# Media attention: fillers on TensorE pinned to program order, and the routing of a row spread over more steps

## The chip, the cores and the metric

The kernel runs on one core of a Trainium2 chip. A core has TensorE (matrix multiply; PE in the profile, and PEld for its weight loads), VectorE (DVE), ScalarE (ACT), GpSimd (POOL) and SyncE (SP, which here only starts DMAs), each with an instruction queue of its own that is worked off in order. The metric is the device time of one execution in microseconds, as the median of several runs.

## The reference

The program is a two-layer decoder on an input of 8 rows (batch entries) of 512 tokens with 256 channels. Six blocks follow one another, each with a residual sum: self-attention, cross-attention, local attention with a feed-forward part, quantized attention, attention to media (a context of 512 tokens), and a mixture of experts. The change concerns the fifth block and the routing of the sixth:

```python
# media attention: 8 heads of 64
xn = (x - mu) * rsqrt(var + eps) * gamma + beta
q = xn @ Wq * scale;  k, v = split(media @ Wkv)
attn = softmax(where(mask, q @ k.T, -inf))
x = x + (attn @ v) @ Wout

# experts: routing of T = 4096 tokens to 8 experts of capacity 512
logits = layernorm(x) @ router_w
expert_idx = argmax(logits);  gate = softmax(logits)[expert_idx]
pos = cumsum(onehot(expert_idx))[token, expert_idx] - 1
keep = pos < 512
expert_in[expert_idx, pos] = layernorm(x) * keep
```

The position of a token inside its expert is a running count over all tokens before it, so the rows are routed one after the other.

## The kernel before, in words

The blocks run as stages. The stage of the change is `stage_media_attention` (line 2745); it takes the eight rows `b` in turn, and beside them, as background work, it routes each finished row to the experts.

**The main line.** A row has 512 queries and 512 keys, and its 8 heads are taken as 4 pairs `c`. The loop at line 2905 goes through 64 steps (its variable is `pair`) and one more to finish, eight to a row, called steps 0 to 7 of a row here; two steps make one pair of heads. In a step, `scores` (matmuls at line 2811) makes the scores of two blocks of 128 keys into two PSUM tiles `sc`, ScalarE takes their exponential (line 2817), and the exponentials are summed over the key blocks into `ma_esum`: GpSimd copies the first (line 2822), VectorE adds the others (line 2824). Then `weigh` (line 2835) multiplies the exponentials of the step before with the values. At the end of an odd pair of heads the sums are added up over the partitions by a matmul (line 2854, `SUM` below), go through DRAM to be inverted and spread (`inverted`, `times_rows`, lines 3163 and 3181), and GpSimd multiplies the output by them (line 3189). After `weigh`, the step runs fillers.

**The fillers.** There are two sources. The generator `prepare` gives the next row's work, one piece at a time: load and layer norm, two transposes (line 2781, `mT`), four projections of the queries (line 2791). The object `later`, of class `Background` (line 3235), holds pieces with a due time. It counts ticks, two to a step, 16 to a row; `later.tick(2)` runs up to two pieces that are due and moves the count on. `later.add(d, f)` makes `f` due `d` ticks from now.

**The routing.** When the output projection of a row (four pieces, line 2892, `PO`) is done, `route` (line 2962) adds its pieces to `later`: `stats` (the write of `x` to the output, and the statistics of the layer norm, lines 143 to 149 and 1460 to 1464), `norm` (four normalizations, line 157, into `mo_rows`; a copy of `x` on GpSimd, line 2982), `turn` twice (four PE transposes each, line 2992, `rT0` and `rT1`, and a copy on ScalarE, line 2995), `logits` (line 3001), `choose` (eight small VectorE operations and one exponential), `count` (two matmuls, lines 3032 and 3033), `place` (thirteen small VectorE operations), and four times `send` (an indirect DMA from GpSimd, line 3064). `count` keeps its PSUM tile until `place` has read it. All fillers on TensorE share two PSUM tiles `pj`.

**What sets the order.** The kernel is written in program order, and the framework that builds it chooses the order of each engine's queue: an instruction that the framework believes to be ready may go ahead of one written before it. `tc.issue_after(ins)` makes whatever its block issues on the engine of `ins` stand behind `ins` in that queue; it is an order and no wait for `ins` to finish. `together` (line 1448) uses it so that the four matmuls of `scores`, `weigh` or `SUM` stand side by side. After the eighth row what is left in `later` is drained, one piece a tick (line 3251), and `stage_moe` (line 3094) loads the first expert's tokens, which the last `send` must have written.

Of the kernel before, what the change touches and what calls it, by code (L numbers as in the profile page):

```python
# [40 lines left out]
B, S, C = 8, 512, 256  # L41
# [1236 lines left out]
class FastDecoder(Decoder):  # L1278
# [164 lines left out]
    def reserve(self, pool, *tiles):  # L1443

        for tag, shape, bufs in tiles:
            self.alloc(pool, shape, F32, tag, bufs=bufs)

    def together(self, n):


        yield 0
        last = next(i for i in reversed(self.nc.cur_bb.bb.instructions) if i.engine == mybir.EngineType.PE)
        with self.tc.issue_after(last), self.tc.high_priority(self.AT_ONCE):
            yield from range(1, n)
# [1290 lines left out]
    def stage_media_attention(self, w, out):  # L2745
# [4 lines left out]
        later = Background()  # L2750
        with self.tc.tile_pool(reuse_waits="tile", name="ma", bufs=2) as pool, self.tc.tile_pool(
# [50 lines left out]
            def scores(n):  # L2802

                b, rest = divmod(n, 8)
                c, kts = rest // 2, (2 * (rest % 2), 2 * (rest % 2) + 1)
                d = held[b]
                both = [self.alloc(psum, [P, 2, 512], F32, "sc", bufs=2) for kt in kts]
                for m in self.together(4):
                    kt, r = kts[m // 2], m % 2
                    rows = slice(64 * r, 64 * r + 64)  # L2810
                    nc.tensor.matmul(  # L2811
                        both[m // 2][:, r, :], d["k"][rows, c, kt * P : (kt + 1) * P], d["q"][rows, c, :],
                        start=True, stop=True,
                    )
                for kt, ps in zip(kts, both):
                    ex = d[4 * c + kt] = self.alloc(pool, [P, 2, 512], F32, "ma_e", bufs=4)
                    nc.scalar.activation(  # L2817
                        ex, ps, AF.Exp, bias=bias[:, b * NST + kt : b * NST + kt + 1], scale=0.125
                    )
                    if kt == 0:  # L2820
                        d["sum", c] = self.alloc(pool, [P, 2, 512], F32, "ma_esum", bufs=3)
                        nc.gpsimd.tensor_copy(d["sum", c], ex)
                    else:
                        nc.vector.tensor_tensor(d["sum", c], d["sum", c], ex, ALU.add)  # L2824
# [80 lines left out]
            for pair in range(0, n + 2, 2):  # L2905
                if pair < n:
                    if pair % 16 == 0:
                        for thunk in ready or ():
                            thunk()
                        ready = prepare(pair // 16 + 1) if pair // 16 + 1 < B else iter(())  # L2910
                    scores(pair // 2)
                if pair >= 2:
                    weigh(pair // 2 - 1)
                for i in (pair, pair + 1):
                    if i % 16 > 0:
                        thunk = next(ready, None)
                        if thunk is not None:
                            thunk()
                    later.tick(2)
            later.drain()  # L2920

    def twice_normal(self, pool, b, kept=None):
# [20 lines left out]
    def routing(self, pool, psum, later, out):  # L2943
# [18 lines left out]
        def route(b):  # L2962
# [26 lines left out]
            def turn(c):  # L2989
                ps = self.alloc(psum, [P, 512], F32, "pj", bufs=2)  # L2990
                for i in range(NST):
                    nc.tensor.transpose(  # L2992
                        ps[:, i * P : (i + 1) * P], d["rows"][:, i, c * P : (c + 1) * P], self.ident
                    )
                nc.scalar.copy(d["xnT"][:, c, :], ps)
# [67 lines left out]
            def send(i):  # L3063
                ins = nc.gpsimd.indirect_dma_start(
                    self.slots, bass.IndirectOffsetOnAxis(ap=d["to"][:, i : i + 1], axis=0),
                    d["rows"][:, i, :], None, bounds_check=NEXP * CAP - 1, oob_is_err=False,
                ).ins

                for other in self.sent:
                    if i == 0:  # L3070
                        self.wait_for(ins, other)
                    else:
                        self.tc.declare_no_dep(ins, other, reason="other slots")
                self.sent = [ins] if i == 0 else self.sent + [ins]

            later.add(1, stats)
            later.add(2, norm)
            later.add(3, lambda: turn(0))
            later.add(4, lambda: turn(1))
            later.add(5, logits)  # L3080
            later.add(6, choose)
            later.add(8, count)
            later.add(9, place)
            for i in range(NST):
                later.add(10 + i, lambda i=i: send(i))

        return route

# [357 lines left out]
```

## Time and profile before

| what | value |
|---|---|
| median of three runs | 3141.81 us (3141.59 to 3142.07) |
| the profiled execution | 3142.42 us |
| its span | 3140.5 us, so 1.9 us lie around it |
| PE busy over the span | 2861.4 us (91%) |
| DVE, ACT, POOL busy | 2156.3, 1146.1, 401.6 us |
| main line of the media stage | 2439.4 to 2863.0 us of the span |
| PE, DVE, ACT, POOL busy there | 403.2, 293.6, 172.4, 106.5 us of 423.6 |
| transposes `rT` there, PE idle ahead of them | 13.2 us in 7 waits |

A busy share is an average over the whole span. The media stage is a stretch of 424 us of it, and its time is read from what TensorE does in this stretch: how long it computes, and what it waits for. An fp32 matmul shows as two records, so four matmuls of `scores` are "x8" in a timeline. Where a group of matmuls starts later than the end of the one before it, the idle time and what ended it stand in brackets.

### The profile page before, as it was taken

To read this page: it belongs to the slowest core of one execution; us is meant where nothing else is said; L and a number is where in the kernel's file an instruction comes from. 1 tells how busy PE (TensorE), PEld (TensorE's weight loads), DVE (VectorE), ACT (ScalarE), POOL (GpSimd) and SP (SyncE) were. 2 spreads that over 40 slices of the span, in tenths; PEclk is the share of its full clock that TensorE was granted. 3 is DMA by queue.
4 is the path that set the end of the run, shared out by engine and by line. 5 is a ranking of instruction groups with operands and counts; after the bars stand their busy time and mean duration, and the time that the engine had idled before them with its cause. 6 is when DMAs were issued, how large, how long until landed. Compare 5 with 4: busy or idle time off the path is not lost. (4 is left out here: it accounts for less than half of the span.)

```text
span 3140.5 us, 40216 instructions
## 1 busy us (share of the span) xinstructions
PE 2861.4 (91%) x14944; PEld 1511.3 (48%) x14944; DVE 2156.3 (69%) x4962; ACT 1146.1 (36%) x1607; POOL 401.6 (13%) x389
## 2 busy tenths in 40 slices
PE   8998889887999999999999999998796999997998
PEld 5652222223555556655555556654444344444665
DVE  7458888887878796356788798648788866656110
ACT  2236656652434431124434431113363434341111
POOL 1111000100110010000110011111201123221111
PEclk9999999989999999999999999999997999998999
DMA  7011111111000001001000011001332122223331
GB/s 238 1 49 48 51 59 47 26 32 47 22 29 15 22 24 42 1 1 35 22 22 15 23 43 61 21 7 61 99 127 93 42 88 95 75 75 97 101 137 60
DMA packets 130696, 168.74 MB, mean 54 GB/s; under 512 B 51760, under 2 KB 79665, under 8 KB 128442
## 3 DMA queue, kind: packets, MB, share of 16 engines
q1 hardware_dynamic: 126394, 154.48, 15.8%
q0 software_dynamic: 4096, 11.59, 1.0%
q8 instruction: 119, 1.95, 0.3%
q14 instruction: 87, 0.71, 0.1%
HBM read 113.12 MB, written 47.50 MB: 51 GB/s over the span
## 5 line engine op out<-in xcount | busy, mean ns | idle before, releaser
L1812 PE MATMUL pj<-w,la_hT 128*128 128x512 f32 x720 | 341.0, 613 | 31.5 <-DVE x L1989 15.5
L1664 DVE TENSOR_TENSOR x_e<-x_e,x_share 128x1024 f32<-128x1024 f32 x256 | 306.8, 1244 | 28.5 <-ACT x_e L1663 27.7
L1663 ACT ACTIVATE x_e<-sc 128x1024 f32<-128x1024 f32 x256 | 249.7, 1025 | 149.8 <-PE sc L1652 147.3
L1812 PEld LDWEIGHTS pj<-w,la_hT 128*128 128x128 f32 x720 | 130.6, 192 | 187.0 <-issue 118.1
L1934 ACT ACTIVATE la_e<-la_e 128x1024 f32<-128x1024 f32 (+1 forms) x128 | 121.1, 953 | 212.0 <-DVE la_e L1930 212.0
L2817 ACT ACTIVATE ma_e<-sc,ma_bias 128x1024 f32<-128x1024 f32 x128 | 135.7, 1110 | 164.9 <-PE sc L2811 163.4
L2143 ACT ACTIVATE lf_gate<-pj,lf_b 128x512 f32<-128x512 f32 (+1 forms) x82 | 56.3, 687 | 347.6 <-PE pj L2122 337.8
L2824 DVE TENSOR_TENSOR ma_esum<-ma_esum,ma_e 128x1024 f32<-128x1024 f32 x96 | 129.1, 1346 | 71.6 <-ACT ma_e L2817 35.6
L1679 PE MATMUL po<-x_e,x_v 128*32 128x512 f32 x1024 | 144.7, 639 | 35.4 <-DVE x_e L1664 33.3
L2122 PE MATMUL pj<-lf_hnT,w 128*128 128x512 f32 (+1 forms) x368 | 171.7, 595 | 1.0 <-DVE lf_hid L2148 1.0
L1930 DVE TENSOR_TENSOR la_e<-sc,la_mask 128x1024 f32<-128x1024 f32 (+1 forms) x128 | 136.9, 1081 | 36.9 <-PE sc L1922 36.8
L1652 PE MATMUL sc<-x_q,x_k 32*128 32x512 f32 x1024 | 160.7, 669 | 0.3 <-ACT x_e L1663 0.2
L3189 POOL TENSOR_TENSOR la_oT<-la_o,x_wide 128x512 f32<-128x512 f32 x64 | 87.3, 1372 | 572.7 <-DMA x_wide<-invs 410.4
L2122 PE MATMUL sc<-lf_hnT,w 128*128 128x512 f32 x336 | 157.9, 592 | 0.0
L2194 PE MATMUL po<-w,lf_hid 128*128 128x256 f32 x640 | 148.8, 379 | 0.0
L2148 DVE SCALAR_TENSOR_TENSOR lf_hid<-sc,lf_b,lf_gate 128x512 f32<-128x512 f32 x70 | 52.4, 748 | 127.2 <-PE sc L2122 127.2
L1922 PE MATMUL sc<-la_qkT 64*128 64x256 f32 (+1 forms) x1024 | 122.8, 370 | 13.1 <-ACT la_qkT L1858 11.3
L1819 ACT ACTIVATE la_sq<-pj 128x512 f32<-128x512 f32 x120 | 71.4, 595 | 169.8 <-PE pj L1812 169.8
L1984 PE MATMUL pj<-w,la_oT 128*128 128x256 f32 x512 | 122.3, 385 | 12.1 <-DVE x L1989 10.2
L2811 PE MATMUL sc<-ma_qT,ma_kT 64*128 64x512 f32 x512 | 129.6, 625 | 0.0
L2194 PEld LDWEIGHTS po<-w,lf_hid 128*128 128x128 f32 x640 | 117.8, 190 | 20.3 <-issue 6.7
L2835 PE MATMUL po<-ma_e,ma_v 128*64 128x512 f32 x512 | 124.3, 606 | 0.0
(491 smaller groups left out, 5297.1 us busy)
## 6 DMA issues: line engine op xcount, KB each, us to landing
x_wide<-invs SPq DMA_DIRECT2D x184, 128.0 KB
w<-in_f_w_dram SPq DMA_DIRECT2D x16, 1024.0 KB
kv<-kv_o SPq DMA_DIRECT2D x56, 256.0 KB
slots<-x_empty SPq DMA_DIRECT2D x8, 1028.0 KB
x_mask<-in_x_maskT_dram SPq DMA_DIRECT2D x8, 1024.0 KB
ma_kT<-kv SPq DMA_DIRECT2D x8, 1024.0 KB
ma_v<-kv SPq DMA_DIRECT2D x8, 1024.0 KB
ex_rows<-slots SPq DMA_DIRECT2D x7, 1028.0 KB
```

The source lines that it names most:

```text
L1652: nc.tensor.matmul(pair[r // 2][:, r % 2, :], d["k"][rows, g, kt * P : (kt + 1) * P], d["q"][rows, e, g, :], start=True, stop=True,)
L1663: nc.scalar.activation(ex, d["e"][rest][p], AF.Exp)
L1664: nc.vector.tensor_tensor(ex, ex, d["share"][:, kt, :].unsqueeze(1).broadcast_to([P, 2, 512]), ALU.mult)
L1679: nc.tensor.matmul(d["po"][32 * r : 32 * r + 32, :], d["v"][:, kt, 8 * g + 2 * r + e, :], ex[r // 2][:, r % 2, :], start=(kt == 0), stop=( ...
L1812: nc.tensor.matmul(ps, d["hT"][:, k, i * P : (i + 1) * P], wqkv[:, k, j * S : (j + 1) * S], start=(k == 0), stop=(k == 1),)
L1930: nc.vector.tensor_tensor(ex[:, :, :n_cols], ps[:, :, :n_cols], mask[:, :n_cols].unsqueeze(1).broadcast_to([P, 2, n_cols]), ALU.add,)
L2122: nc.tensor.matmul(ps[:m, :], w1[:, k, at : at + m], held[b]["hnT"][:, k, :], start=(k == 0), stop=(k == 1))
L2194: nc.tensor.matmul(ps[:, :C], held[b]["hid"][:, f, i * P : (i + 1) * P], w2[:, f, :], start=(f == 0), stop=False,)
L2811: nc.tensor.matmul(both[m // 2][:, r, :], d["k"][rows, c, kt * P : (kt + 1) * P], d["q"][rows, c, :], start=True, stop=True,)
L2817: nc.scalar.activation(ex, ps, AF.Exp, bias=bias[:, b * NST + kt : b * NST + kt + 1], scale=0.125)
L2824: nc.vector.tensor_tensor(d["sum", c], d["sum", c], ex, ALU.add)
L2835: nc.tensor.matmul(d["po"][64 * r : 64 * r + 64, :], d["v"][:, kt, 128 * c + 64 * r : 128 * c + 64 * r + 64], exs[m // 2][:, r, :], start= ...
```

## The change

There are two edits. First, `in_turn` is `issue_after` on the newest TensorE instruction that has been written; in the loop each piece of `prepare` and each `later.tick(2)` runs inside it. A filler's TensorE instructions then never stand ahead of the `scores` and `weigh` of their own step. What is written later may still go ahead of them. The final `later.drain()` is not inside it.

Second, for rows 0 to 5 the pieces of `route` become due later: `turn`, `logits` and `choose` by 2 ticks (one step), and `count`, `place` and `send` by 4 ticks (two steps). `stats` and `norm` keep their due times, and rows 6 and 7 keep all of theirs.

```diff
+    def newest(self, engine):
+        return next(i for i in reversed(self.nc.cur_bb.bb.instructions) if i.engine == engine)
+
+    def in_turn(self):
+        return self.tc.issue_after(self.newest(mybir.EngineType.PE))
...
                     if i % 16 > 0:
                         thunk = next(ready, None)
                         if thunk is not None:
-                            thunk()
-                    later.tick(2)
+                            with self.in_turn():
+                                thunk()
+                    with self.in_turn():
+                        later.tick(2)
             later.drain()
...
+            slow = 2 if b < B - 2 else 0
             later.add(1, stats)
             later.add(2, norm)
-            later.add(3, lambda: turn(0))
-            later.add(4, lambda: turn(1))
-            later.add(5, logits)
-            later.add(6, choose)
-            later.add(8, count)
-            later.add(9, place)
+            later.add(3 + slow, lambda: turn(0))
+            later.add(4 + slow, lambda: turn(1))
+            later.add(5 + slow, logits)
+            later.add(6 + slow, choose)
+            later.add(8 + 2 * slow, count)
+            later.add(9 + 2 * slow, place)
             for i in range(NST):
-                later.add(10 + i, lambda i=i: send(i))
+                later.add(10 + 2 * slow + i, lambda i=i: send(i))
```

## The prediction

> **What bounds the kernel now.** I read the page first, then the busy time of the media stage alone, then who TensorE waited for in it, and last the order of events around one wait. Page, part 1:
>
> ```profile
> span 3140.5 us, 40216 instructions
> PE 2861.4 (91%) x14944; PEld 1511.3 (48%) x14944; DVE 2156.3 (69%) x4962; ACT 1146.1 (36%) x1607; POOL 401.6 (13%) x389
> ```
>
> Nothing outside the media stage is edited, so only this stage counts. Busy times by stretch (after the window: its length, then PE, PEld, DVE, ACT, POOL, granted clock, DMA share, GB/s); the first is the stage's main line, the other two are short stretches in it:
>
> ```profile
> 2439.40:2863.00 423.60, 403.19 (x1737) 170.63 (x1736) 293.59 (x698) 172.44 (x195) 106.51 (x98) 0.99 0.22 72
> ...
> 2527.50:2530.90 3.40, 3.40 (x10) 0.99 (x8) 1.40 (x2) 1.83 (x3) 0.00 (x0) 0.51 0.01 2
> ...
> 2746.00:2749.40 3.40, 3.40 (x10) 1.73 (x12) 2.02 (x4) 0.58 (x1) 0.00 (x0) 0.50 0.02 5
> ```
>
> TensorE computes 403.2 of 423.6 us, so it is the bound and leaves 20.4 us idle; two stretches of 3.4 us ran at half clock. The waits of PE in this window:
>
> ```profile
> PE pj L2992 <- DVE mo_rows L157: 13.2, 7, 2.4
> PE sum L2876 <- DVE ma_esum L2824: 4.1, 1, 4.1
> PE pj L2781 <- DVE ma_xn L157: 2.0, 1, 2.0
> PE pj L2791 <- DVE ma_qT L103: 1.1, 2, 0.8
> ```
>
> They add up to the 20.4 us. 13.2 of it is one wait: `rT0`, the first routing transposes of a row, for the normalized rows; seven times, 2.1 to 2.4 us for rows 0 to 5 and 0.25 for row 6. The timeline of TensorE at row 0's:
>
> ```profile
> 2519.79 1.99 PE L2811 MATMUL sc<-ma_qT,ma_kT 64*128 64x512 f32 x8
> 2521.71 1.94 PE L2835 MATMUL po<-ma_e,ma_v 128*64 128x512 f32 x8
> 2525.81 1.30 PE L2992 MATMUL pj<-ident,mo_rows 128*128 128x128 f32 x4 [2.16 <-DVE mo_rows L157]
> 2527.04 3.34 PE L2811 MATMUL sc<-ma_qT,ma_kT 64*128 64x512 f32 x8
> 2530.31 2.23 PE L2835 MATMUL po<-ma_e,ma_v 128*64 128x512 f32 x8
> 2532.47 0.66 PE L2992 MATMUL pj<-ident,mo_rows 128*128 128x128 f32 x4
> 2532.97 0.29 PE L3001 MATMUL pj<-mo_wr,mo_xnT 128*128 128x8 f32 x2
> 2533.18 1.99 PE L2811 MATMUL sc<-ma_qT,ma_kT 64*128 64x512 f32 x8
> 2535.10 1.73 PE L3001 MATMUL pj<-mo_wr,mo_xnT 128*128 128x8 f32 x14
> 2536.76 1.94 PE L2835 MATMUL po<-ma_e,ma_v 128*64 128x512 f32 x8
> ```
>
> Scores, values, then `rT0` stalls, and the next scores, which need nothing from it, stand behind. The order is already the program's: fillers follow the values of their step. I went through the other rows so; only the first row's `mT` (2.0 us idle) stands ahead of the scores of its step. The same stall at row 1, on VectorE:
>
> ```profile
> 2578.45 1.14 DVE L1460 TENSOR_SCALAR mo_ln_rstd<-mo_ln_var 128x4 int32<-128x4 int32 x1
> ...
> 2582.17 1.38 DVE L157 TENSOR_SCALAR mo_rows<-x,mo_ln_mean,mo_ln_rstd 128x256 f32<-128x256 f32 x4
> 2583.47 1.22 DVE L2824 TENSOR_TENSOR ma_esum<-ma_esum,ma_e 128x1024 f32<-128x1024 f32 x1
> ```
>
> VectorE worked without a break from the last piece of `x` (2576.80) to the end of the normalizations (2583.55): it isn't blocked, TensorE arrives too early, at 2580.5.
>
> **What the Trainium skill says.** *Perfetto Trace Analysis*, Sequencer Loop: an instruction waits for its semaphore in its engine's queue. The trace agrees: the scores at 2527.04 are behind the 2.16 us. *TensorE: Matmul & The Clock Gate*, What's actually happening: the clock is halved after a too idle window of about 3.4 us, free-running. The trace agrees on length and ratio (3.40 us at 0.51), and that it is a matter of phase: of rows 0 to 5, rows 0 and 4 were hit. *SBUF — State Buffer*, SBUF: two separate sides: VectorE and GpSimd share a port pair that one holds for a whole instruction. The trace fits: the small operation at 2578.45 took 1.14 us beside a 1.28 us multiply that GpSimd began at 2578.28; the same one at 2849.82 took 0.17.
>
> **The change part by part.** I counted due times by hand with the two-per-tick limit.
>
> *Routing spread.* Row 0's `norm` stays at step 6 of the next row, `rT0` goes from step 6 to step 7. The later `send` pieces take tick places, so that from row 1 on `PO` ends one tick later, `stats` and `norm` drift to the end of steps 6 and 7, and `rT0` falls into step 0 of the row after, behind its `SUM`. What each stall costs now, from starts in the timeline: idle 13.2 − 0.25 = 12.95 us for the six; transposes 1.23 instead of 0.50 us (2527.04 − 2525.81, 2532.97 − 2532.47), six times 0.73 = 4.4; the half-clock stretches, row 0: scores 3.27 instead of 1.92, values 2.16 instead of 1.87, 1.6 together; row 4 the same way 1.2. Sum 20.1 us.
>
> Does `rT0` find its rows then? Row 0: without the stall TensorE reaches it one step (1.92 + 1.87) after 2523.6, at 2527.4. VectorE began to normalize at 2525.3, and four take 1.38: 2526.7. No wait, 0.7 us to spare. Row 1: from 2576.7, three times scores and values (3 × 3.79) brings `SUM` at 2588.1 and `rT0` at 2589.1. VectorE must by then have done 6.75 us (2576.80 to 2583.55) and three sum additions (1.22 + 2.55): 10.5 of 11.3 us to `SUM`. The slack is 0.8 us, so I leave 0.5 us a row as residue: 3.0 us.
>
> The moved pieces issue the same instructions: 8 transposes, 16 logits records, 4 count records, 21 small VectorE operations, four `send` of about 1.27 us start to start on GpSimd. `choose` and `place` now stand with the next row's `mT` and behind its projections, where VectorE has about 6.5 of 6.7 us in step 1; today `place` is there, and the projections wait 1.1 us in all. I take no change; ends −1.1 (gone) to +3 (0.5 us for each of six rows). On GpSimd, `send` falls behind line 3189's multiplies instead of ahead of them. Queued behind it is the copy of line 2822, for which the VectorE additions wait; today they wait 33.2 us in all for that copy, under cover of TensorE's scores, and without this cover a 1.27 us `send` would cost as much. On SP only the write of `x` moves, later, when `x` is long done. Rows 1 to 5 invert half of their sums a tick later; half a row lies before their use. Zero for these.
>
> *Fillers in turn.* The first row's `mT` goes behind its step's scores and values. These can start when the exponentials are done, about 1.4 us after the first scores instead of after the 2.0 us idle and 1.4 us of transposes; the transposes (1.0 us warm) follow. Gain 0.9 us; ends 0 to 2.0. Elsewhere it only repeats the order.
>
> *The end of the stage.* The 4.1 us wait of row 7's sum, plus 1.7 us of clock behind it, comes when row 5's `send` hold GpSimd back and its copies and multiplies then come in one burst (2827.8 to 2831.2) that shuts VectorE out. The `send` now come later, but `place` of row 5 falls there; I take half, 2.9 us; ends 0 to 5.8. Row 6's `logits` (1.9 us) are pinned behind row 7's output projection, so `choose` and `place` of row 6 run in the last routing chain, and row 7's first `send` waits for row 6's to land (2.3 to 6.8 us). I take 1.0 us of loss; ends −1.1 to +6.
>
> Sum: −20.1 + 3.0 + 0 − 0.9 − 2.9 + 1.0 = −19.9 us. Against 3142.4 us of the profiled execution (span 3140.5 and 1.9 around it) that is 3122.5; the median of the runs is 0.6 us lower: 3122.
>
> **The rivals.** (1) The wait only changes place: VectorE is so full at the row's turn that `SUM` or `rT0` waits about 2 us again. For it: 10.5 of 11.3 us. Then 1.5 us more for each of six rows, 9 us of the gain is lost: 3131. (2) Slower: GpSimd shuts VectorE out in that window. Two multiplies (line 3189) of 1.27 us, a copy of 1.04 and a `send` of 1.27 landing there would add 4.85 us to the 10.5 and make `SUM` 4.1 us late; with the 0.73 and 0.5 us that follow a stall today, 5.3 us a row. It decides from 20.1 / 6 = 3.4 us a row; at 5.3 the gain becomes a loss of 6 × 1.9 = 12: 3154. Against it: the burst occurred once, at row 7. (3) The edits do nothing, 3142: the queues were in program order already, and the stall would have to follow `norm` in its drift; but the piece and its input move apart by a step of 3.8 us.
>
> **How the numbers follow.** The forecast 0.70, rival (1) 0.14, rival (2) 0.09, rival (3) 0.07. The forecast's own ends are 3112 (all 20.1, 2.0 at the start, 1.1, 5.8 and 1.1 gained: −30) and 3130 (a residue of 1 us a row and 6 us lost in the last routing, the rest as taken: −12). The range, 3112 to 3135, takes in rival (1) and leaves out the others. A measurement can tell 0.2%, 6.3 us: faster than 3135.5 are the forecast and nearly all of (1), 0.83; slower than 3148.1 most of (2), 0.08; the rest 0.09.
>
> **What would show it.** Right: the wait of line 2992 falls from 13.2 us to under 3, PE idle in the stage under 10 us, fewer half-clock stretches, transposes 0.5 us for four, and a main line some 20 us shorter while all later stages only shift. Wrong: a new PE wait for `ma_esum` at line 2854 or for `ma_xnT` at line 2791; or the stretch from the last values to the first expert, 37 us now, longer by more than the stage gains.

## The result, and the profile after

The median of 14 runs is 3131.93 us (3123.72 to 3137.76), beside 3141.94 us of the kernel before on the same chip. The ratio is 0.9964, 95% interval 0.9951 to 0.9977: by the ratio a gain of 11.3 us, a little over half of the forecast. The profiled execution took 3135.97 us. Its page, part 1:

```profile
span 3133.9 us, 40202 instructions
PE 2859.4 (91%) x14929; PEld 1512.2 (48%) x14944; DVE 2158.6 (69%) x4962; ACT 1145.6 (37%) x1607; POOL 402.9 (13%) x389
```

The work is the same. The time of one execution varies by some 10 us ahead of the media stage: the stage's first scores start anywhere between 2433.5 and 2443.0 us in the ten traces of this study. I therefore measure the stage itself, from its first scores to its last scores, and from there to the first expert's transposes (starts in the timelines). Behind that point all traces have 242.8 to 243.6 us left, so the later stages only shift.

| kernel | first to last scores | last scores to first expert | sum |
|---|---|---|---|
| before | 414.9 | 43.2 | 458.1 |
| after | 401.4 | 46.1 | 447.5 |

The stage became 10.5 us shorter: 13.5 gained in the loop, 2.9 lost at its end. Busy times by stretch (columns as before: length, PE, PEld, DVE, ACT, POOL, granted clock, DMA share, GB/s), of the main line and of its last 48.5 us, row 7:

```profile
2443.00:2852.00 409.00, 398.12 (x1717) 167.12 (x1716) 291.33 (x695) 171.93 (x195) 112.57 (x98) 0.99 0.22 75
...
2804.50:2853.00 48.50, 42.54 (x184) 18.59 (x180) 36.88 (x68) 17.44 (x21) 11.58 (x11) 0.93 0.13 44
```

TensorE is idle for 10.9 us of the first window where it was 20.4, and ran below full clock only in its last row. The waits of PE in it:

```profile
PE pj L2899 <- POOL ma_oT L3200: 4.1, 1, 4.1
PE sum L2861 <- DVE ma_esum L2831: 3.0, 5, 0.7
PE pj L2798 <- DVE ma_xnT L2791: 1.8, 1, 1.8
PE pj L2899 <- DVE x L2904: 0.7, 2, 0.5
PE sc L2818 <- ACT ma_e L2824: 0.4, 1, 0.4
```

One more wait stands just behind the window, in the stretch from the last scores to the first expert, where the kernel before had none:

```profile
2853.03 1.08 PE L2883 MATMUL sum<-ma_esum,ones 128*64 128x512 f32 x4 [1.85 <-DVE ma_esum L2831]
```

The 13.2 us at `rT0` (now line 3001) are gone altogether. Three others stand in their place: row 7's output projection waits 4.1 us for GpSimd, where row 7's sum waited 4.1 us for VectorE; `SUM` waits five times for `ma_esum`; and the first row's projections wait for their transposed input. The timeline of TensorE at one of the five, in row 4 (the first line is an undisturbed `SUM`, for comparison):

```profile
2563.11 1.06 PE L2861 MATMUL sum<-ma_esum,ones 128*32 128x512 f32 x8
...
2637.36 1.94 PE L2842 MATMUL po<-ma_e,ma_v 128*64 128x512 f32 x8
2639.22 1.05 PE L2861 MATMUL sum<-ma_esum,ones 128*32 128x512 f32 x4
2640.85 1.05 PE L2861 MATMUL sum<-ma_esum,ones 128*32 128x512 f32 x4 [0.58 <-DVE ma_esum L2831]
2641.84 1.09 PE L3001 MATMUL pj<-ident,mo_rows 128*128 128x128 f32 x8
```

`rT0` and `rT1`, eight transposes, stand behind `SUM` as the forecast had it, at 0.5 us for four and without a wait. But `SUM` has changed. Undisturbed, its four matmuls stand side by side, eight records in 1.06 us. Here the last two wait 0.58 us, and the two halves take 1.05 us each: 2.68 us from 2639.22 to 2641.90. The wait is 0.58 us, its cost 1.62. The five cost 1.59 to 1.69 us each, 8.2 us together.

Why `ma_esum` is late is seen on VectorE and GpSimd just before (first VectorE, then GpSimd):

```profile
2629.11 1.24 DVE L148 COPY mo_ln_mean<-mo_ln_mv 128x4 f32<-128x4 f32 x1
2630.27 0.15 DVE L149 TENSOR_SCALAR mo_ln_var<-mo_ln_mv 128x4 f32<-128x4 f32 x1
2630.46 0.89 DVE L1467 TENSOR_SCALAR mo_ln_rstd<-mo_ln_var 128x4 int32<-128x4 int32 x1
2631.39 1.19 DVE L1469 SCALAR_TENSOR_TENSOR mo_ln_t<-mo_ln_rstd 128x4 f32<-128x4 f32 x1
2632.61 0.94 DVE L1470 TENSOR_TENSOR mo_ln_t<-mo_ln_t,mo_ln_var 128x4 f32<-128x4 f32 x1
2633.59 0.17 DVE L1471 SCALAR_TENSOR_TENSOR mo_ln_rstd<-mo_ln_t,mo_ln_rstd 128x4 f32<-128x4 f32 x1
...
2634.98 1.38 DVE L157 TENSOR_SCALAR mo_rows<-x,mo_ln_mean,mo_ln_rstd 128x256 f32<-128x256 f32 x4
2636.28 5.66 DVE L2831 TENSOR_TENSOR ma_esum<-ma_esum,ma_e 128x1024 f32<-128x1024 f32 x4
```

```profile
2629.07 1.27 POOL L3200 TENSOR_TENSOR ma_oT<-ma_o,x_wide 128x512 f32<-128x512 f32 x1 [7.22 <-DMA x_wide<-invs]
2630.28 1.04 POOL L2991 COPY mo_rows<-x 128x1024 f32<-128x1024 f32 x1
2631.30 1.26 POOL L3200 TENSOR_TENSOR ma_oT<-ma_o,x_wide 128x512 f32<-128x512 f32 x1
2632.51 1.03 POOL L2829 COPY ma_esum<-ma_e 128x1024 f32<-128x1024 f32 x1
```

GpSimd does four operations in a row, and in each of the four one small operation of VectorE is held until it ends: 1.24, 0.89, 1.19 and 0.94 us, where outside the burst each takes 0.16 to 0.17 us. That is 4.26 us for some 0.7 us of work, so about 3.6 us lost. The normalization and then the sum additions start late by as much, and `SUM` finds the last addition unfinished. This fits *SBUF — State Buffer*, SBUF: two separate sides, of the Trainium skill: a GpSimd operation and a VectorE operation (in a two-port mode, or with two inputs in SBUF) need one port pair, and whichever starts first holds it for its whole instruction.

Row 7, where the longest wait is (TensorE, then GpSimd):

```profile
2829.21 1.22 PE L2899 MATMUL pj<-w,ma_oT 128*128 128x256 f32 x2 [4.14 <-POOL ma_oT L3200]
2830.36 3.68 PE L2842 MATMUL po<-ma_e,ma_v 128*64 128x512 f32 x8
```

```profile
2811.37 1.27 POOL L3200 TENSOR_TENSOR ma_oT<-ma_o,x_wide 128x512 f32<-128x512 f32 x1
...
2822.46 1.28 POOL L3073 DMA_INDIRECT slots<-mo_rows,mo_to  x1 [1.77 <-DVE mo_to L3070]
...
2827.75 1.41 POOL L3200 TENSOR_TENSOR ma_oT<-ma_o,x_wide 128x512 f32<-128x512 f32 x1
```

Of the two multiplies of the last pair of heads, one ran at 2811.37. The other stood behind the four `send` of row 5, of which the first waits for its positions `mo_to`. `PO` needs both multiplies. After the wait the values took 3.68 us instead of 1.87, at half clock.

### The profile page after: what moved, and what is told of

It is laid out like the page before. It is cut to its first block, busy times and chain, and to the rows that moved or that the text cites. A ratio compares the mean times of both kernels' runs of the same rounds, so it can differ in the third digit from the quotient of the medians.

```text
span 3133.9 us, 40202 instructions
## 1 busy us (share of the span) xinstructions
PE 2859.4 (91%) x14929; PEld 1512.2 (48%) x14944; DVE 2158.6 (69%) x4962; ACT 1145.6 (37%) x1607; POOL 402.9 (13%) x389
## 5 line engine op out<-in xcount | busy, mean ns | idle before, releaser
L2831 DVE TENSOR_TENSOR ma_esum<-ma_esum,ma_e 128x1024 f32<-128x1024 f32 x96 | 121.6, 1271 | 58.9 <-ACT ma_e L2824 30.0
L1929 PE MATMUL sc<-la_qkT 64*128 64x256 f32 (+1 forms) x1024 | 123.3, 371 | 13.0 <-ACT la_qkT L1865 11.3
```

## The experiments

The theory after the result: the gain that is missing is lost where work moved by drift. `tick(2)` runs at most two due pieces a tick; the pieces delayed by one or two steps push each other and `stats`, `norm` and the multiplies later, into crowded places. The rivals: the pinning of the fillers costs it, or VectorE is simply too full.

**One edit alone.** The spreading without the pinning, and the pinning without the spreading:

```diff
-                            with self.in_turn():
-                                thunk()
-                    with self.in_turn():
-                        later.tick(2)
+                            thunk()
+                    later.tick(2)
```

> The changed kernel without its first edit: fillers are not pinned, the routing is spread. TensorE's queue then differs from the changed kernel's in one place, the first row's two mT pieces, which stand ahead of the second scores again. Theory: all of the gain is the spread; 3132 us, within 2 us of the changed kernel, first row 40.1 us from its first scores to the next row's instead of 40.5, rest of the stage as in the changed kernel. Rival (the pinning is what took the stalls away): the waits for the routing transposes come back, 13 us of them, and the time is 3142.

```diff
-            slow = 2 if b < B - 2 else 0
+            slow = 0
```

> The kernel before with the first edit alone: fillers pinned, routing not spread. TensorE's queue differs from the kernel before's only in the first row's mT. Theory (the first edit is worth nothing here): stage 458 us within 1 us, first row 40.5 us, six waits of 2.1 us at the routing transposes stay. Rival (it carries part of the gain): the waits fall under 10 us in all.

Spreading alone: 3132.06 us, ratio 0.9966 (0.9955 to 0.9977); stage 401.7 + 45.6 = 447.3 us. That is the whole result, with the same waits (2.9 us in five at `SUM`, 4.2 at the output projection), and an end that is 2.5 us longer than before (2.9 with both edits). Pinning alone, one run: 3140.3 us, stage 417.0 + 43.2 = 460.2 us, 2.1 us longer than before in this trace, with the waits of the kernel before:

```profile
PE pj L3001 <- DVE mo_rows L157: 13.4, 7, 2.4
PE sum L2883 <- DVE ma_esum L2831: 4.1, 1, 4.1
PE pj L2798 <- DVE ma_xnT L2791: 1.8, 1, 1.8
```

So the pinning gains nothing. It exchanges the first row's 2.0 us wait of `mT` for 1.8 us of the projections and 0.4 of the scores, and pins no filler to a costly place. Of the 2.1 us only 0.6 are idle time; the rest is computing, and of rows 0 to 5 three have a stretch at half clock in this trace where the kernel before had two. So single traces of the stage can differ by some 2 us for such a reason.

**The burst, from both sides.** Take one of the four operations out of GpSimd's burst, by giving the copy of `x` to ScalarE:

```diff
-                nc.gpsimd.tensor_copy(rows[:, :, C : 2 * C], x)
+                nc.scalar.copy(rows[:, :, C : 2 * C], x)
```

> The changed kernel with the copy of x into mo_rows on ScalarE instead of GpSimd (1.04 us a row). Theory (GpSimd's burst of four operations shuts VectorE out of the norm chain for 3.5 us a row, and the sum additions behind it come 0.6 us too late for SUM): VectorE gets about 0.9 us a row back, the five waits of 0.55 to 0.65 us at SUM fall to near 0, and with the split matmuls 1.6 us each, some 8 us come back: 3124 us. Rival (VectorE has too much to do by itself, or the additions wait for GpSimd's copy of the first exponentials): the waits at SUM stay at 0.5 us or more, time 3132 within 2 us.

Or leave GpSimd and put the VectorE instructions of `norm` behind the additions that are already written:

```diff
+            def norm_behind():
+                with self.tc.issue_after(self.newest(mybir.EngineType.DVE)):
+                    norm()
...
-            later.add(2, norm)
+            later.add(2, norm_behind)
```

> The changed kernel with one more order edge: the four normalizations of a row stand on VectorE behind the newest VectorE instruction written before them, which puts the three sum additions of the row's last two steps ahead of them. Theory (only the order on VectorE makes SUM wait, the transposes have slack): SUM waits 0 us instead of 3.0 in all; the transposes rT0 wait up to 0.5 us a row; 8 us less than the changed kernel at no wait, 5 us less with 0.5 us a row: 3124 to 3128. Rival (VectorE's total is too much, the wait only goes back to the transposes): 1 us or more a row of waiting at rT0, 3132 within 2 us.

With the copy on ScalarE no row's `SUM` shows a wait any more, and the stage is 395.2 + 45.6 = 440.8 us, 6.7 less than after. The rows don't gain the whole price: four of the five `SUM` still take 1.85 to 1.99 us instead of 1.06, such as this one.

```profile
2637.38 1.85 PE L2861 MATMUL sum<-ma_esum,ones 128*32 128x512 f32 x8
```

The second half starts some 0.8 to 0.9 us late, but while the first still runs, so no idle time shows. With `norm` behind the additions, one `SUM` of the five is still long (1.96 us), four are 1.06 to 1.07, and the stage is 394.6 + 46.1 = 440.7 us, the same gain. The burst on GpSimd and the order on VectorE are thus both needed for the loss; either can be taken away. The 4 us wait of row 7 for GpSimd stays in both (4.1 and 3.8), and so does the longer end, so these have another cause. By the runs the two are 3130.72 us (ratio 0.9955, 0.9941 to 0.9969) and 3129.46 us (0.9956, 0.9940 to 0.9973). That is only 1.3 and 2.6 us below spreading alone on the same chip, both miss the expected times, and the first lies where its rival had it. Their intervals overlap with that of the change. So that the waits go is shown; the 6.7 us rest on one trace each.

**The limit of two pieces a tick.** If drift is behind all of it, a third piece a tick must take away all of it:

```diff
-                        later.tick(2)
+                        later.tick(3)
```

> The changed kernel with up to three pieces a tick instead of two. No piece is displaced by a send any more: the inversion of half of the sums, the output projection, stats and norm keep the ticks of the kernel before, rT0 stands in step 7 and rT1 and logits in step 0, and row 6's logits stand ahead of row 7's last values as in the kernel before. Theory (the drift through the limit of two makes the GpSimd burst late and the end longer): the waits at SUM fall under 1 us in all, from the last scores to the first expert 43 us instead of 46, 3121 to 3125 us. Rival (the drift gives rT0 its slack): rT0 waits again, 1 us or more a row, and the time is 3132 or more.

3117.85 us (3115.5 to 3121.3), ratio 0.9913 (0.9892 to 0.9934); stage 389.9 + 43.2 = 433.1 us, 14.4 less than after. That is below the expected range. The waits of PE:

```profile
PE pj L2798 <- DVE ma_xnT L2791: 1.8, 1, 1.8
PE pj L3001 <- DVE mo_rows L157: 1.0, 2, 0.7
PE sc L2818 <- ACT ma_e L2824: 0.4, 1, 0.4
```

`SUM` waits nowhere, row 7's wait for GpSimd is gone, and the end is as long as before the change. On GpSimd both multiplies of row 7 now come together, ahead of the four `send`:

```profile
2807.41 2.51 POOL L3200 TENSOR_TENSOR ma_oT<-ma_o,x_wide 128x512 f32<-128x512 f32 x2 [2.23 <-DMA x_wide<-invs]
...
2815.94 1.28 POOL L3073 DMA_INDIRECT slots<-mo_rows,mo_to  x1 [1.77 <-DVE mo_to L3070]
```

The burst, though, is not gone. In rows 0 to 5 the twelve small operations of the layer norm (from the copy to the last `rstd`) still take 4.6 to 5.6 us together; in rows 1 to 5 after the change they take 5.5 to 5.6, and where GpSimd holds none of them (row 3 of the spreading alone) 1.9. So it wasn't the drift that brought the burst. What frees `SUM` here, as far as the trace shows, is that `rT0` again stands ahead of it, which gives VectorE more time, and that in rows 2, 4 and 5 less is held; how much each of the two is worth was not separated.

The same limit in the kernel before, as a control on whether the limit alone does it:

> The kernel before with up to three pieces a tick and nothing else: the control for the run with three pieces. Theory (the limit only costs where the spread routing makes pieces collide, in the kernel before hardly any do): the waits of 2.1 us at the routing transposes stay, the stage takes 458 us as in the kernel before, within 3 us, 3142 us. Rival (three pieces are a gain of their own, about 14 us): 444 us, 3128 us.

3155.98 us, ratio 1.0044 (1.0027 to 1.0060), stage 430.2 + 43.2 = 473.4 us: slower, and by far more than either theory allowed. The stall at `rT0` grew:

```profile
PE pj L2992 <- DVE mo_rows L157: 17.9, 7, 3.8
```

Six of the seven are now 2.7 to 3.8 us, and a stretch at half clock follows each of the six: at row 0 the idle time is 2.85 us, and the scores behind it take 3.59 us instead of 1.92. Of the 15.4 us that the stage is longer, 4.7 are idle time and the rest is computing (the loop before, then with the limit alone):

```profile
2439.40:2854.30 414.90, 394.49 (x1691) 166.48 (x1690) 286.20 (x691) 168.56 (x190) 106.51 (x98) 0.99 0.22 74
2433.50:2863.70 430.20, 405.06 (x1691) 169.62 (x1690) 290.31 (x691) 169.23 (x190) 107.48 (x98) 0.96 0.21 71
```

The longer wait doesn't come from TensorE's queue: between the last piece of the output projection and `rT0` stand the scores and values of one step, 3.8 us, as before. It comes from the burst, which here holds three or four operations of the layer norm instead of two (in row 3 a third in part). Row 3, the longest wait, first before and then with the limit alone:

```profile
2687.64 1.13 DVE L1460 TENSOR_SCALAR mo_ln_rstd<-mo_ln_var 128x4 int32<-128x4 int32 x1
2688.80 0.93 DVE L1462 SCALAR_TENSOR_TENSOR mo_ln_t<-mo_ln_rstd 128x4 f32<-128x4 f32 x1
2689.77 0.16 DVE L1463 TENSOR_TENSOR mo_ln_t<-mo_ln_t,mo_ln_var 128x4 f32<-128x4 f32 x1
```

```profile
2688.89 1.23 DVE L1460 TENSOR_SCALAR mo_ln_rstd<-mo_ln_var 128x4 int32<-128x4 int32 x1
2690.15 0.94 DVE L1462 SCALAR_TENSOR_TENSOR mo_ln_t<-mo_ln_rstd 128x4 f32<-128x4 f32 x1
2691.12 1.19 DVE L1463 TENSOR_TENSOR mo_ln_t<-mo_ln_t,mo_ln_var 128x4 f32<-128x4 f32 x1
2692.35 0.94 DVE L1464 SCALAR_TENSOR_TENSOR mo_ln_rstd<-mo_ln_t,mo_ln_rstd 128x4 f32<-128x4 f32 x1
```

So the limit is worth something only together with the spreading, which keeps `rT0` away.

The wider limit and `norm` behind the additions (for rows 0 to 5) together:

> The changed kernel with up to three pieces a tick and, for rows 0 to 5, the normalizations behind the sum additions on VectorE: both repairs at once. Theory (two separate causes of the waits at SUM, each removed by either repair): little is left to win, the stage from its first scores to the first expert 432 to 434 us as with three pieces alone (433.1), 3116 to 3119 us. Rival (the order on VectorE is a gain of its own): 6 us or more less, 426 to 427 us. Loss possible: rT0 stands one step after norm here, so rows that come behind the additions can stall it, up to 1 us a row, 439 us.

3122.66 us, ratio 0.9942 (0.9923 to 0.9961), stage 394.5 + 43.2 = 437.7 us: 4.6 us worse than the limit alone. `rT0` stands one step behind `norm`, and waits 2.7 us in all for it, in four rows, where the limit alone left 1.0. Where the drift is gone the additions needn't go first.

**Row 5 alone.** If row 7's wait and the longer end come from row 5's late pieces, it is enough to give row 5 its old due times:

```diff
-            slow = 2 if b < B - 2 else 0
+            slow = 2 if b < B - 3 else 0
```

> The changed kernel with row 5 given the due times of the kernel before, rows 0 to 4 spread. Theory (the 4.1 us wait at row 7's output projection and the 2.9 us longer end come from row 5's send and row 6's logits, both late through row 5's drift): from the last scores to the first expert 43.2 us again instead of 46.1; the 4.1 us wait for line 3200's multiply goes, the wait of the kernel before for the sums (4.1 us) may take its place. Row 5's first routing transposes stall again, 2 us. Stage 443 to 449 us. Rival (the longer end has its cause in row 7's own chain): 46 us stay.

One run: 3129.45 us, stage 401.8 + 43.2 = 445.1 us. The wait for GpSimd is gone, the end is 43.2 us again, and in exchange the old wait of row 7 is back:

```profile
PE sum L2883 <- DVE ma_esum L2831: 4.2, 1, 4.2
```

As expected. The longer end is row 5's drift, and the wait of row 7 has two forms: with early `send` VectorE is late, with late `send` GpSimd is.

## Why the prediction was right in its sign and half right in its size

The direction and the range held; the likeliest time did not. The range held only because it took in rival (1): the forecast's own ends were 3112 and 3130 us, and 3131.93 lies beyond them. Of its signs of being right the lost wait of `rT0` came, and TensorE's idle time of 10.9 us just missed the limit of 10; both signs of being wrong that it named in the loop came, the waits for `ma_esum` at `SUM` and for `ma_xnT`. In the stage, forecast against measured (us):

| step of the prediction | forecast | measured |
|---|---|---|
| *Routing spread*: the stalls and what follows them | −20.1 | −20.1 |
| its residue | +3.0 | +8.2 |
| moved pieces | 0 | −0.4 |
| *Fillers in turn* | −0.9 | +0.4 |
| *The end of the stage*: row 7's stall | −2.9 | +0.9 |
| *The end of the stage*: row 6's `logits` | +1.0 | +1.4 |
| sum | −19.9 | −9.6 |

The measured column is worked out from the traces. The stalls are entered whole, since all three parts are gone (next paragraph). The residue is the excess of the five `SUM` over 1.06 us. The moved pieces are 1.1 us of waits gone and 0.7 come. The start is the length of row 0, 40.51 less 40.13 us. Row 7's stall is 4.14 us of wait and 2.5 of half clock, less 5.8. The last is 2.9 us less the 1.5 that only moved behind the last scores. The stage as a whole measured −10.5; 0.9 us of that I can assign to no step.

**The stalls: size right, one reading behind it wrong.** Line 3001 waits nowhere in the main line, eight transposes take 1.02 us start to start, and the granted clock from row 1 to the beginning of row 7 is 1.00 (317.25 us busy of 320.90). That setting the transposes later in the order takes the stall away was right too, and the run with the spreading alone shows it. But the reading that VectorE "isn't blocked" was wrong. In rows 0 to 5 of the kernel before, the twelve small operations take 3.9 to 4.2 us, some 2.0 to 2.3 us of it held by GpSimd; the prediction itself shows one of them, 1.14 us instead of 0.17. And in all eighteen stalls of these rows (the kernel before, the pinning alone, the limit alone) TensorE's wait is the time of these twelve less 1.75 to 1.85 us: 3.93 us and a wait of 2.09 in row 1 before, 5.59 and 3.76 in row 3 with the limit alone. Unheld they take 1.94 us (row 3 of the spreading alone), which by estimate would leave a stall of about 0.1 us. So keeping GpSimd away from the layer norm in the kernel before is a rival to the spreading, and no run tried it.

**The residue: mechanism right, size wrong, and this is the largest miss.** The step found the crowded place, `SUM` behind VectorE. Two terms failed. VectorE's 10.5 of 11.3 us held about 2.0 us lost to GpSimd; in the changed kernel GpSimd's burst holds four operations of the layer norm instead of two and takes 3.6. The 1.6 more use up the slack of 0.8 and leave 0.8 us. And the residue of 0.5 us a row was priced as the wait alone. The wait was 0.55 to 0.65 us, close to that, but it falls between the halves of `SUM`, so that they no longer lie side by side, and costs 1.6. *TensorEngine Tiling (Array Packing)*, Key Properties, of the Trainium skill says that different tiles can execute in parallel. The trace agrees: four in 1.06 us, two alone in 1.05. A wait between them therefore costs its own length and one whole half, 1.0 us. Rival (1) had this wait at 2 us: its mechanism was a third as long. That its time, 3131, came out is luck: the residue cost 5.2 us more than forecast and not 9, and row 7, the start and the end made up the rest.

**The moved pieces: right.** `choose` and `place` beside the projections cost nothing; the projections' former 1.1 us went, and 0.7 us came for `x` at the output projection.

***Fillers in turn*: wrong sign.** The step let the transposes of `mT` follow the scores and stopped there. The projections behind them need their result by way of VectorE (line 2791), and waited 1.8 us. That wait was hidden before, because scores and values stood between; whoever moves a producer back moves it nearer to its consumer.

***The end of the stage*, row 7: wrong.** The step let half of the stall go, because `send` comes later. I named the right queue, and in "*moved pieces*" even that `send` would stand behind the multiplies of line 3189. In row 7 it stood between them: the second multiply ended up behind four `send`. The stall was as long, 4.1 us, and the clock behind it cost 2.5 us instead of 1.7 (`PO` 1.22 instead of 0.5, values 3.68 instead of 1.87). That the drift reaches the multiplies was in my count of due times ("Rows 1 to 5 invert half of their sums a tick later") and priced at zero for rows 1 to 5, and not at all for row 7.

***The end of the stage*, row 6's `logits`: size about right, reason wrong.** The `logits` did go behind row 7's output projection (they start at 2863.13, it at 2854.04). The stretch from the last scores grew by 2.9 us, of which 1.5 are row 6's first transposes and the wait ahead of them, which stood ahead of the last scores before. But the step called the `logits` pinned, and the kernel without any pinning has them there too, while three kernels with it (pinning alone, the wider limit, and row 5 early) don't. It is drift again: row 5's late pieces push row 6's.

**Rivals (2) and (3)** did not come. The burst that rival (2) feared did come in that window, but without a `send` in it, and it added 1.6 us to what VectorE lost before instead of 4.85. Rival (2) decides from 3.4 us a row; the burst cost 1.6.

## What to carry to other kernels

When pieces of background work are delayed under a limit per tick, they delay the pieces that were not touched: list where each piece ends up, its GpSimd and VectorE instructions too, and price every one that changes its neighbours. Before moving work on TensorE, see whether the engine that it waits for is itself held up: here small operations of VectorE that took some six times their usual time were in plain view in the first trace. Try the limit together with the spreading: here, in the stage, the spreading gave 10.8 us, the limit in the old order lost 15.4, and both together gained 25.0, the fastest kernel of the study (ratio 0.9913). A wait is priced by what it separates, and not by its length alone.

## What the runs showed of the hardware that was not expected

- A wait of 0.55 to 0.65 us between matmuls that normally lie side by side costs 1.6 us; even one too short to be shown made four of the five `SUM` 1.85 to 1.99 us long instead of 1.06.
- A burst on GpSimd held up to one small VectorE instruction for each of its operations: instructions of 0.16 to 0.17 us took 0.89 to 1.24 us, and four GpSimd operations lost VectorE 3.6 us.
- Stalls of 2.1 to 2.4 us were followed by half clock in two of six rows of the kernel before and in three of six with the pinning alone; stalls of 2.7 to 3.8 us, in the kernel with the limit alone, in six of six.
